# The first 40 microseconds of a two-layer graph kernel: ScalarE normalizes twelve tiles, one token load moves up, and five of GpSimd's loads wait

## The chip, the cores and the metric

The kernel runs on one core of one Trainium2 chip. The core has a matrix engine (TensorE, PE in the profile), a vector engine (VectorE, DVE), a scalar engine (ScalarE, ACT), GpSimd (POOL), a queue engine that only issues transfers here (SyncE, SP), and 16 DMA engines that all transfers share. The metric is the device time of one execution in microseconds (us), lower is better.

## The reference

Two layers are applied to 3327 nodes with 256 features. Each layer has a graph part and a mixture of experts. Only the first graph part matters here:

```python
x = x + relu(adj @ (layernorm(x) @ W) + b)          # layer 0, graph part
x = x + moe0(layernorm(x))                          # top 2 of 8 experts, hidden 1024, relu
x = x + gnn1(layernorm(x), adj)                     # tanh-filtered adjacency, two projections
x = x + moe1(layernorm(x))                          # top 2 of 8 experts, hidden 256, gelu

def layernorm(x, eps=1e-5):
    return (x - mean(x)) / sqrt(var(x) + eps)       # over the 256 features of a node
```

All of it is in float32. `adj` is 3327 x 3327, 44 MB, and is the largest input.

## The kernel before

The nodes are padded to 3328, which is 26 tiles of 128. `x` holds all tiles in SBUF, and `s` holds their normalized copy. The transposed adjacency is read in 13 panels of 256 columns, each in two chunks of 13 tiles (1664 KB); six ring buffers take the chunks. Layer 0 multiplies in the order (adj @ normalized x) @ W. For a panel, TensorE accumulates over the 26 tiles two matmuls per tile (`add`, L381 to L389, one for each half of the features), ScalarE copies the two sums out (L410), TensorE multiplies by W (L396, in `finish`), and VectorE adds the bias `gnn_b_sb` and the residual (`add_relu`, L329 and L330). Then `after0` normalizes the panel's two tiles and routes them to experts, using `gate` (L447).

The first two panels are computed side by side, so that the start has two panels' work for every tile of tokens that arrives: L424 to L426 run over the first 13 tiles and, for each, over both panels. The profile counts two records for each float32 matmul, so a tile with both panels has eight.

**The start.** SP issues the loads in the order of the code: L147 to L153 load the tokens in five groups (tiles 0 and 1, 2 and 3, 4 to 7, 8 to 12, 13 to 25), and behind each of the first four groups the slices of the first chunk of panels 0 and 1 for the same tiles. Next come the second chunks of both panels (L344), W (L417), the gate weights, which are written to DRAM turned (L143), and the chunks of panel 2. Meanwhile 54 small bf16 matmuls run on TensorE (L160).

**Normalizing.** L1111 to L1113 go through six groups of tiles, (0, 2), (2, 2), (4, 4), (8, 4), (12, 6) and (18, 8), each given as first tile and number of tiles. For a group, `statistics` (L267) takes mean and variance of each tile (L275, L276) and then 1/sqrt by a guess and three Newton steps on very short operands (L278 to L287); `layernorm` (L290) then writes each tile of `s` with one VectorE instruction (L297). A group's tiles are ready only after the statistics of all its tiles. The tile framework's scheduler orders the instructions of an engine by priority; `behind` (L231) and `tc.issue_after` set that priority only, they add no wait on the chip. Each engine then works in the order it was given, and each instruction waits by semaphores for its inputs.

**ScalarE at the start.** Apart from the copies it only counts the positive entries of the adjacency: `count` (L1121) runs eight sign instructions per chunk (L1126, 128x416), the first of which waits for the whole first chunk of panel 0.

**GpSimd at the start.** It makes constants and issues six loads: the bias on all partitions (`gnn_b_sb`, 128 KB, L245, called at L253), `f0_bg_sb` (4 KB, L254), and for layer 1 `g1_wg_sb` (256 KB, L1116), `f1_r_sb` (8 KB), `f1_b1_sb` (8 KB) and `g1_bp_sb` (1 KB). Then follow the zeros that `fill` (L1085) needs, and the load of `gate`, 1 MB, each partition getting a copy (L258), which waits until the turned weights are in DRAM. The profile shortens some of the names (`g_wg_sb`, `f_bg_sb`).

Of the kernel before, what the change touches and what calls it, by code (L numbers as in the profile page):

```python
# [10 lines left out]
F32 = mybir.dt.float32  # L11
BF16 = mybir.dt.bfloat16
I32 = mybir.dt.int32
AF = mybir.ActivationFunctionType
ALU = mybir.AluOpType
# [7 lines left out]
P = 128  # L23
NT = 26
NP = NT * P
D = 256
DC = D // P
E = 8
# [4 lines left out]
CJ = NT // NCHUNK  # L33
# [58 lines left out]
def gnn_moe_two_layers(  # L92
# [24 lines left out]
    nc = tc.nc  # L117

    const = ctx.enter_context(tc.tile_pool(name="const", bufs=1))
    state = ctx.enter_context(tc.tile_pool(name="state", bufs=1))  # L120
    work = ctx.enter_context(tc.tile_pool(name="work", bufs=3))
# [5 lines left out]
    x = state.tile([P, NT, D], F32, name="x")  # L127
    s = state.tile([P, NT, D], F32, name="s")
# [5 lines left out]
    def piece(pan, k):  # L134
        return ring[(pan * NCHUNK + k) % RING].rearrange("p (c w) -> p c w", w=PW)
# [4 lines left out]
    def turn_gate(w):  # L140
        g = dram.tile([E, D], F32, name=f"gate{len(gates)}")
        with nc.allow_non_contiguous_dma("a few thousand elements"):
            d = nc.sync.dma_start(out=g.rearrange("e d -> d e"), in_=w)  # L143
        gates.append(g)
        return d

    for t, n in [(0, 2), (2, 2), (4, 4), (8, CJ - 8), (CJ, NT - CJ)]:  # L147
        nc.sync.dma_start(out=x[:, t : t + n, :], in_=x_in[:, t : t + n, :])
        if t < CJ:
            for pan in range(2):  # L150
                nc.sync.dma_start(
                    out=piece(pan, 0)[:, t : t + n, :], in_=adjT[pan, 0, :, t : t + n, :]
                )  # L153

    ones_sq = const.tile([P, P], BF16, name="ones_sq")
    nc.gpsimd.memset(ones_sq, 1.0)
# [2 lines left out]
    for _ in range(WARM):  # L159
# [9 lines left out]
        out=before,  # L169
        in_=before,  # L170
# [56 lines left out]
    def follow(later, earlier):  # L227
        for o in earlier:
            tc.add_manual_dep(later.ins, o.ins.name, after, reason="same rows of DRAM")

    def behind(instructions):  # L231

        if instructions and any(i is instructions[-1].ins for i in nc.cur_bb.bb.instructions):
            return tc.issue_after(instructions[-1].ins)
        return nullcontext()

    def by_feature(name, w, t=None):
        if t is None:
            t = const.tile([P, DC, w.shape[1]], F32, name=name)
        nc.gpsimd.dma_start(out=t, in_=w.rearrange("(c p) n -> p c n", p=P))  # L240
        return t

    def on_all_partitions(name, b):
        t = const.tile([P, b.shape[1]], F32, name=name)
        nc.gpsimd.dma_start(out=t, in_=b.partition_broadcast(P))  # L245
        return t

    def plain(name, a):
        t = const.tile(list(a.shape), F32, name=name)
        nc.gpsimd.dma_start(out=t, in_=a)  # L250
        return t

    gnn_b_sb = on_all_partitions("gnn_b_sb", g0_b[0:1, :])  # L253
    f0_bg_sb = on_all_partitions("f0_bg_sb", f0_bg[0:1, :])  # L254
    gate = state.tile([P, E, D], F32, name="gate")

# [8 lines left out]
    last_normalized = []  # L265

    def statistics(t0, n, kept=None):  # L267


        mv, guess = kept or (  # L270
            work.tile([P, n, 2], F32, name="ln_mv"), work.tile([P, n], I32, name="ln_guess")
        )
        for g in range(n):
            st = work.tile([P, 6], F32, name="ln_st")
            nc.vector.bn_stats(out=st, in_=x[:, t0 + g, :])  # L275
            nc.vector.bn_aggr(out=mv[:, g, :], in_=st)  # L276
        ve = work.tile([P, n], F32, name="ln_ve")
        nc.vector.tensor_scalar(ve, mv[:, :, 1], EPS, None, ALU.add)  # L278
        nw = work.tile([P, n], F32, name="ln_nw")
        half = nw.bitcast(I32)  # L280
        nc.vector.tensor_scalar(half, ve.bitcast(I32), 1, None, ALU.logical_shift_right)
        nc.vector.tensor_scalar(guess, half, -1.0, float(0x5F3759DF), ALU.mult, ALU.add)
        rs = guess.bitcast(F32)
        for _ in range(3):
            nc.vector.scalar_tensor_tensor(nw, rs, -0.5, rs, ALU.mult, ALU.mult)
            nc.vector.tensor_tensor(nw, nw, ve, ALU.mult)
            nc.vector.scalar_tensor_tensor(rs, nw, 1.5, rs, ALU.add, ALU.mult)  # L287
        return mv, rs

    def layernorm(t0, n, stats=None, at=0, xn=None):  # L290


        mv, rs = stats or statistics(t0, n)
        if xn is None:
            xn = work.tile([P, n, K, RW], F32, name="xn")
        for g in range(n):
            last_normalized[:] = [nc.vector.tensor_scalar(  # L297
                xn[:, g, 0, 0:D], x[:, t0 + g, :], mv[:, at + g, 0:1], rs[:, at + g : at + g + 1],
                ALU.subtract, ALU.mult,
            )]  # L300
        return xn
# [24 lines left out]
    def add_relu(x_tile, ps, b_sb):  # L326

        t = work.tile([P, D], F32, name="gnn_t", bufs=2)
        nc.vector.tensor_tensor(t, ps, b_sb, ALU.add)  # L329
        nc.vector.scalar_tensor_tensor(x_tile, t, 0.0, x_tile, ALU.max, ALU.add)  # L330
# [8 lines left out]
    def load_panel(pan, prepare, earlier=(), begun=0):  # L339

        for k in range(begun, NCHUNK):
            a = piece(pan, k)
            with behind(earlier):
                d = nc.sync.dma_start(out=a, in_=adjT[pan, k])  # L344
            last_piece[:] = [d]
            prepare(pan, k, a)
# [24 lines left out]
    def aggregate_first(b_sb, w, w_sb, begin, count, after):  # L371

        sums, waiting, copied = {}, [], []

        def start(pan):
            sums[pan] = [psy.tile([P, PW], F32, name="ps_g", tag="py") for _ in range(DC)]

        def add(pan, j):  # L381
            for c in range(DC):
                nc.tensor.matmul(  # L383
                    sums[pan][c],
                    lhsT=s[:, j, ts(c, P)],
                    rhs=piece(pan, j // CJ)[:, j % CJ, :],
                    start=(j == 0),
                    stop=(j == NT - 1),
                )  # L389

        def finish():
            pan, g = waiting.pop()
            for it in range(PW // P):
                ps = psh.tile([P, D], F32, name="ps_o", tag="ph")
                for c in range(DC):
                    nc.tensor.matmul(  # L396
                        ps, lhsT=g[:, c, ts(it, P)], rhs=w_sb[:, c, :], start=(c == 0),
                        stop=(c == DC - 1),
                    )
                add_relu(x[:, pan * (PW // P) + it, :], ps, b_sb)  # L400
            after(pan)

        def rest(pan, first):
            for j in range(first, NT):
                add(pan, j)
                if waiting and j == first + BEHIND:
                    finish()
            g = work.tile([P, DC, PW], F32, name="xnT", bufs=2)
            for c in range(DC):
                copied.append(nc.scalar.copy(g[:, c, :], sums[pan][c]))  # L410
            waiting.append((pan, g))

        loaded = RING // NCHUNK
        for pan in range(loaded):
            load_panel(pan, lambda pan, k, a: None, begun=1 if pan < 2 else 0)
            if pan == 1:
                nc.sync.dma_start(out=w_sb, in_=w.rearrange("(c p) n -> p c n", p=P))  # L417
                with tc.issue_after(last_piece[0].ins):
                    turn_gate(f0_wgT)
        with tc.issue_after(last_piece[0].ins):  # L420
            turn_gate(f1_rT)
        for pan in range(2):
            start(pan)
        for j in range(CJ):  # L424
            for pan in range(2):
                add(pan, j)  # L426
        for pan in range(NPAN):
            if pan > 1:
                start(pan)
            if loaded < min(pan + RING // NCHUNK, NPAN):  # L430
                load_panel(loaded, lambda pan, k, a: None)
                loaded += 1
            begin(pan)
            count(pan, copied)
            rest(pan, CJ if pan < 2 else 0)
        return finish
# [648 lines left out]
    def fill(*lists):  # L1085


        with tc.issue_after(last_piece[0].ins):
# [13 lines left out]
            for xlist in lists:  # L1102
                for e in range(E):
                    first = xlist[e * NP : e * NP + SB, :].rearrange("(g p) d -> p g d", p=P)
                    nc.sync.dma_start(out=first[:, :, 0:ID], in_=zeros)
                    with nc.allow_non_contiguous_dma("two elements of a partition"):
                        nc.sync.dma_start(
                            out=first[:, :, ID : ID + 1], in_=rows_f[:, e, :].unsqueeze(2)
                        )

    for t0, n0 in [(0, 2), (2, 2), (4, 4), (8, 4), (12, 6), (18, 8)]:  # L1111
        with behind(last_normalized if t0 < 12 else ()):
            layernorm(t0, n0, xn=s[:, t0 : t0 + n0, :].unsqueeze(2))  # L1113

    with tc.issue_after(last_normalized[0].ins):
        g1_wg_sb = by_feature("g1_wg_sb", g1_wg)  # L1116
        f1_r_sb = by_feature("f1_r_sb", f1_rT)
        f1_b1_sb = plain("f1_b1_sb", f1_b1)
        g1_bp_sb = plain("g1_bp_sb", g1_bp)

    def count(pan, copied):  # L1121
        for k in range(NCHUNK):
# [463 lines left out]
```

## Time and profile before

| | us |
|---|---|
| runs shown, median of 4 | 1233.91 (1232.66 to 1238.42) |
| the profiled execution's own time | 1236.28 |
| its span | 1234.6 |
| TensorE busy in the span | 1196.3 (97%) |
| VectorE, ScalarE, GpSimd busy | 708.4, 511.6, 271.1 |
| first float32 matmul | 7.69 |
| tile 12's first matmul | 33.05 |
| W multiplied into panel 0 (first L396) | 51.28 |

Times inside the profile count from the start of the span. A line of the view in order of time gives start, length, engine, source line, operation, the tiles written and read, how often, and in brackets how long the engine had been idle and what it waited for. A line of the view by stretches gives the length, then for PE, PEld (weight loads), DVE, ACT and POOL the busy time and the number of instructions, then the granted TensorE clock (1.00 is full), the share of time in which the 16 DMA engines were busy (which can read a little over 1), and GB/s.

### The profile page before, as it was taken

Reading aid. Unit: us, or ns where it says so; the run is one execution under the profiler, and the core shown is the slowest. Engines: PE = TensorE matmul, PEld = TensorE weight load, DVE = VectorE, ACT = ScalarE, POOL = GpSimd, SP = SyncE. Lnnn points to the kernel's source line nnn. Section 1 sums busy time; section 2 is a strip of 40 time slices with the busy share of each in tenths; the row PEclk is TensorE's granted clock in tenths of the full one; section 3 lists DMA queues with packets and bytes.
Section 4 is the critical chain, followed back from the end, with each engine's and each line's share of the span. In section 5 each row is a group of like instructions: output and inputs, shape, how many; then the busy total and the mean of one; then the engine's idle time right before and its main releaser. Section 6 shows DMA issues by size and latency. Waiting matters only on the chain. (4 is left out here: it accounts for less than half of the span.)

```text
span 1234.6 us, 18156 instructions
## 1 busy us (share of the span) xinstructions
PE 1196.3 (97%) x5819; PEld 1035.4 (84%) x5819; DVE 708.4 (57%) x2841; ACT 511.6 (41%) x950; POOL 271.1 (22%) x341
## 2 busy tenths in 40 slices
PE   8999999999999999999999999999999999989973
PEld 7888888888888888888888888888888888868863
DVE  7577756766682111211111358389999998785454
ACT  2655456446322222223232325994554551033321
POOL 3004112211231111110111110013233232255531
PEclk9999999999999999999999999999999999989986
DMA  9799744443357556657575746234554451568686
GB/s 341 178 310 276 212 163 152 162 165 124 111 191 237 184 189 199 232 177 259 179 248 189 277 168 265 101 138 174 184 178 163 172 199 50 157 191 247 206 267 214
DMA packets 123178, 241.60 MB, mean 196 GB/s; under 512 B 24480, under 2 KB 93120, under 8 KB 116160
## 3 DMA queue, kind: packets, MB, share of 16 engines
q1 hardware_dynamic: 108656, 205.59, 51.2%
q0 software_dynamic: 11136, 31.60, 7.0%
q10 hardware_dynamic: 3280, 3.15, 0.7%
q8 instruction: 48, 0.79, 0.3%
q14 instruction: 58, 0.48, 0.1%
HBM read 203.98 MB, written 36.33 MB: 195 GB/s over the span
## 5 line engine op out<-in xcount | busy, mean ns | idle before, releaser
L383 PE MATMUL ps_g<-ring,s 128*128 128x256 f32 x1352 | 297.0, 381 | 4.3 <-DVE s L297 4.3
L360 PE MATMUL ps_g<-s,ring 128*128 128x256 f32 x1352 | 294.2, 380 | 0.0
L383 PEld LDWEIGHTS ps_g<-ring,s 128*128 128x128 f32 x1352 | 257.0, 191 | 40.1 <-DVE s L297 5.3
L360 PEld LDWEIGHTS ps_g<-s,ring 128*128 128x128 f32 x1352 | 256.0, 190 | 34.4
L941 PE MATMUL ps_h<-xT,ring 128*128 128x256 f32 (+1 forms) x1176 | 252.8, 368 | 4.3 <-ACT xT L932 4.0
L941 PEld LDWEIGHTS ps_h<-xT,ring 128*128 128x128 f32 x1176 | 207.3, 192 | 41.9 <-ACT xT L932 4.4
L948 ACT ACTIVATE wide<-ps_h,ring 128x256 f32<-128x256 f32 (+1 forms) x240 | 110.1, 459 | 285.3 <-PE ps_h L941 265.4
L447 DVE SCALAR_TENSOR_TENSOR rt_product<-xn,gate 128x256 f32<-128x256 f32 x400 | 198.6, 496 | 12.2
L980 PE MATMUL ps_y<-ring,wide 128*128 128x256 f32 x896 | 200.3, 379 | 0.0
L551 POOL DMA_INDIRECT xlist<-xn,rt_idx x104 | 105.1, 1011 | 390.8 <-DVE ln_ve L278 154.0
L980 PEld LDWEIGHTS ps_y<-ring,wide 128*128 128x128 f32 x896 | 167.1, 190 | 21.0
L1126 ACT ACTIVATE sign<-ring,below 128x416 bf16<-128x416 f32 x208 | 133.5, 642 | 9.7 <-DMA ring<-in_adjT 3.5
L551 POOL DMA_INDIRECT ys<-narrow,index x56 | 54.8, 978 | 326.8 <-DVE narrow L988 234.7
L1275 ACT ACTIVATE ring<-ring 128x3328 f32<-128x3328 f32 x22 | 65.4, 2979 | 87.7 <-DVE ring L1274 50.6
L932 DVE COPY xT<-ptb 128x512 f32<-128x512 f32 (+1 forms) x29 | 18.9, 651 | 142.1 <-PE ptb L929 142.1
L987 DVE TENSOR_TENSOR narrow<-ps_y,ring 128x256 f32<-128x256 f32 x56 | 23.8, 424 | 131.7 <-PE ps_y L980 130.3
L512 ACT ACTIVATE rt_d<-rt_d 128x2 f32<-128x2 f32 x26 | 5.3, 203 | 164.2 <-DVE rt_d L511 164.1
L551 POOL DMA_INDIRECT ys<-wide,index x58 | 58.5, 1008 | 67.1 <-DVE wide L988 36.0
L1276 ACT ACTIVATE ring<-ring 128x3328 f32<-128x3328 f32 x22 | 65.4, 2979 | 0.6
L329 DVE TENSOR_TENSOR gnn_t<-ps_o,gnn_b_sb 128x256 f32<-128x256 f32 x26 | 11.0, 424 | 82.4 <-PE ps_o L396 82.4
L980 PE MATMUL ps_y<-s,narrow 128*128 128x256 f32 (+1 forms) x200 | 50.3, 392 | 2.8 <-issue 2.7
L275 DVE BATCH_NORM_STATS2 ln_st<-x 128x6 f32<-128x256 f32 x104 | 42.1, 414 | 6.1 <-DMA x<-in_x 5.5
(213 smaller groups left out, 1039.3 us busy)
## 6 DMA issues: line engine op xcount, KB each, us to landing
ring<-in_adjT SPq DMA_DIRECT2D x50, 1664.0 KB
ring<-in_f_w1T SPq DMA_DIRECT2D x30, 1024.0 KB
ring<-in_f_w2T SPq DMA_DIRECT2D x30, 1024.0 KB
ring<-xlist SPq DMA_DIRECT2D x52, 258.0 KB
ring<-in_f_w SPq DMA_DIRECT2D x36, 256.0 KB
ring<-ys SPq DMA_DIRECT2D x12, 512.0 KB
ring<-in_f_b SPq DMA_DIRECT2D x34, 128.0 KB
xlist<-wide SPq DMA_DIRECT2D x16, 257.0 KB
```

Source lines behind the costliest of these rows:

```text
L275: nc.vector.bn_stats(out=st, in_=x[:, t0 + g, :])
L360: nc.tensor.matmul(ps[it], lhsT=chunks[k][:, c, ts(it, P)], rhs=s[:, j, :], start=(j == 0), stop=(j == NT - 1),)
L383: nc.tensor.matmul(sums[pan][c], lhsT=s[:, j, ts(c, P)], rhs=piece(pan, j // CJ)[:, j % CJ, :], start=(j == 0), stop=(j == NT - 1),)
L447: nc.vector.scalar_tensor_tensor(product, xn[:, g, 0, 0:D], 1.0, gate[:, e, :], ALU.mult, ALU.mult, accum_out=sc[:, g, e : e + 1],)
L551: d = nc.gpsimd.indirect_dma_start(out=a[:, :], out_offset=bass.IndirectOffsetOnAxis(ap=index, axis=0), in_=rows_, in_offset=None,)
L941: nc.tensor.matmul(ps, lhsT=w1[:, c, ts(hc, P)], rhs=xT[:, c, :], start=(c == 0), stop=(c == DC - 1),)
L948: nc.scalar.activation(hT[:, hc, :], ps, func, bias=bb1[:, hc : hc + 1])
L980: last_product[:] = [nc.tensor.matmul(ps, lhsT=hT[:, hc, ts(g, P)], rhs=w2[:, hc, :], start=(hc == 0), stop=(hc == hc_n - 1),)]
L987: nc.vector.tensor_tensor(y[:, g, :], ps, bb2, ALU.add)
L1126: nc.scalar.activation(sign, piece(pan, k)[:, :, ts(i, GROUP)], AF.Sign, bias=below, accum_out=positive[:, pan, i, k : k + 1],)
L1275: nc.scalar.activation(a, a, AF.Square)
L1276: nc.scalar.activation(a, a, AF.Tanh)
```

## The change

There are four edits, all in the first 55 us.

1. SP's order: the tokens of tiles 2 and 3 are issued ahead of panel 1's first slice instead of behind it. Everything else keeps its place.
2. TensorE's order: over the first 13 tiles, panel 0 takes two tiles, then panel 1 takes the same two.
3. For tiles 0 to 11, VectorE computes only the statistics and, once per group, a shift of -mean/std; ScalarE writes the tiles of `s` as scale times x plus shift. Tiles 12 to 25 stay on VectorE. The first ScalarE instruction brings the load of its function table with it, which now waits for the first tokens instead of the adjacency. In ScalarE's order three sign instructions stand between tiles 4 to 7 and tiles 8 to 11, the other five of that chunk behind them.
4. GpSimd's loads: `gnn_b_sb`, `g1_wg_sb`, `f1_r_sb`, `f1_b1_sb` and `g1_bp_sb` get a true dependence on the last normalization instruction of the start (that of tile 25). On GpSimd's queue they now stand behind the `gate` load, in this order, and ahead of the copies for the first token lists. `f0_bg_sb` stays where it was; the zeros of `fill` come earlier.

```diff
-    for t, n in [(0, 2), (2, 2), (4, 4), (8, CJ - 8), (CJ, NT - CJ)]:
+    def load_tokens(t, n):
         nc.sync.dma_start(out=x[:, t : t + n, :], in_=x_in[:, t : t + n, :])
-        if t < CJ:
-            for pan in range(2):
-                nc.sync.dma_start(
-                    out=piece(pan, 0)[:, t : t + n, :], in_=adjT[pan, 0, :, t : t + n, :]
-                )
+    def load_slice(pan, t, n):
+        nc.sync.dma_start(out=piece(pan, 0)[:, t : t + n, :], in_=adjT[pan, 0, :, t : t + n, :])
+
+    first_groups = [(0, 2), (2, 2), (4, 4), (8, CJ - 8), (CJ, NT - CJ)]
+    load_tokens(*first_groups[0])
+    for group, following in zip(first_groups, first_groups[1:]):
+        load_slice(0, *group)
+        if group[0] == 0:
+            load_tokens(*following)
+        load_slice(1, *group)
+        if group[0] > 0:
+            load_tokens(*following)
...
-    gnn_b_sb = on_all_partitions("gnn_b_sb", g0_b[0:1, :])
+    gnn_b_sb = const.tile([P, D], F32, name="gnn_b_sb")
     f0_bg_sb = on_all_partitions("f0_bg_sb", f0_bg[0:1, :])
...
-        for j in range(CJ):
+        for j in range(0, CJ, 2):
             for pan in range(2):
-                add(pan, j)
+                for i in range(j, min(j + 2, CJ)):
+                    add(pan, i)
...
     for t0, n0 in [(0, 2), (2, 2), (4, 4), (8, 4), (12, 6), (18, 8)]:
-        with behind(last_normalized if t0 < 12 else ()):
+        if t0 >= 12:
             layernorm(t0, n0, xn=s[:, t0 : t0 + n0, :].unsqueeze(2))
-    with tc.issue_after(last_normalized[0].ins):
-        g1_wg_sb = by_feature("g1_wg_sb", g1_wg)
-        f1_r_sb = by_feature("f1_r_sb", f1_rT)
-        f1_b1_sb = plain("f1_b1_sb", f1_b1)
-        g1_bp_sb = plain("g1_bp_sb", g1_bp)
+            continue
+        with behind(last_shift):
+            mv, rs = statistics(t0, n0)
+            shift = work.tile([P, n0], F32, name="ln_shift")
+            last_shift[:] = [nc.vector.scalar_tensor_tensor(
+                shift, mv[:, :, 0], -1.0, rs, ALU.mult, ALU.mult
+            )]
+        for g in range(n0):
+            nc.scalar.activation(
+                s[:, t0 + g, :], x[:, t0 + g, :], AF.Identity, bias=shift[:, g : g + 1],
+                scale=rs[:, g : g + 1],
+            )
+    for t, w in [
+        (gnn_b_sb, g0_b[0:1, :].partition_broadcast(P)),
+        (g1_wg_sb, g1_wg.rearrange("(c p) n -> p c n", p=P)),
+        (f1_r_sb, f1_rT.rearrange("(c p) n -> p c n", p=P)),
+        (f1_b1_sb, f1_b1),
+        (g1_bp_sb, g1_bp),
+    ]:
+        follow(nc.gpsimd.dma_start(out=t, in_=w), last_normalized)
```

More of the change, by code (lines that the diff above doesn't have):

```diff
@@ L1109, in fill @@
                         )
+    last_shift = []
     for t0, n0 in [(0, 2), (2, 2), (4, 4), (8, 4), (12, 6), (18, 8)]:
-        with behind(last_normalized if t0 < 12 else ()):
+        if t0 >= 12:
             layernorm(t0, n0, xn=s[:, t0 : t0 + n0, :].unsqueeze(2))
-    with tc.issue_after(last_normalized[0].ins):
-        g1_wg_sb = by_feature("g1_wg_sb", g1_wg)
-        f1_r_sb = by_feature("f1_r_sb", f1_rT)
-        f1_b1_sb = plain("f1_b1_sb", f1_b1)
-        g1_bp_sb = plain("g1_bp_sb", g1_bp)
+            continue
[10 more added lines that the diff above has]
+            )
+    g1_wg_sb = const.tile([P, DC, D], F32, name="g1_wg_sb")
+    f1_r_sb = const.tile([P, DC, E], F32, name="f1_r_sb")
+    f1_b1_sb = const.tile(list(f1_b1.shape), F32, name="f1_b1_sb")
+    g1_bp_sb = const.tile(list(g1_bp.shape), F32, name="g1_bp_sb")
+    for t, w in [
[6 more added lines that the diff above has]
+        follow(nc.gpsimd.dma_start(out=t, in_=w), last_normalized)
     def count(pan, copied):
```

## The prediction

> **What bounds the kernel now.** Read first the busy shares on the page, then who waits for whom, then the first 100 us in order of time, since every edit lies in the first 55 us.
>
> ```profile
> PE 1196.3 (97%) x5819; PEld 1035.4 (84%) x5819; DVE 708.4 (57%) x2841; ACT 511.6 (41%) x950; POOL 271.1 (22%) x341
> ...
> PE ps_g L383 <- DVE s L297: 4.3, 3, 2.1
> ...
> POOL gate L258 <- DMA gate<-in_f_wgT: 30.1, 1, 30.1
> ```
>
> TensorE is the bound. The edits can reach only its start and the three waits for a normalized tile, 4.3 us together. TensorE in order of time (start, length, what, and in brackets the idle time before):
>
> ```profile
> 1.07 4.71 PE L160 MATMUL ps_warm<-ones_sq 128*128 128x128 bf16 x54 [1.07 <-POOL ones_sq L156]
> 7.69 3.72 PE L383 MATMUL ps_g<-ring,s 128*128 128x256 f32 x16 [1.90 <-DVE s L297]
> 13.54 19.22 PE L383 MATMUL ps_g<-ring,s 128*128 128x256 f32 x80 [2.14 <-DVE s L297]
> 33.05 18.40 PE L383 MATMUL ps_g<-ring,s 128*128 128x256 f32 x84 [0.28 <-DVE s L297]
> ```
>
> 16 records are tiles 0 and 1 for both panels, 80 are tiles 2 to 11, and at 33.05 TensorE gets tile 12. After that it has no idle time until far behind panel 0's finish, so **whatever tile 12 gains, the kernel gains**. VectorE says what tile 12 waits for:
>
> ```profile
> 9.70 0.75 DVE L275 BATCH_NORM_STATS2 ln_st<-x 128x6 f32<-128x256 f32 x2 [1.74 <-DMA x<-in_x]
> ...
> 13.08 0.74 DVE L297 TENSOR_SCALAR s<-x,ln_mv,ln_guess 128x256 f32<-128x256 f32 x2
> ...
> 26.31 0.76 DVE L275 BATCH_NORM_STATS2 ln_st<-x 128x6 f32<-128x256 f32 x2 [1.31 <-DMA x<-in_x]
> ...
> 32.58 0.73 DVE L297 TENSOR_SCALAR s<-x,ln_mv,ln_guess 128x256 f32<-128x256 f32 x2
> ```
>
> The last tokens (tiles 13 to 25) land at 26.31; tile 12, one of their group of six, is ready 6.74 us later. VectorE was idle before them, so the transfer decides, not VectorE. TensorE in 13.54 to 32.76 had time to lose: ten tiles at 8 records of 0.217 us (104 take 22.61) are 17.4 us, and they took 19.2, because the clock was halved for a stretch. The stretches around it (length, busy time and count per engine, clock, DMA share, GB/s):
>
> ```profile
> 5.00:6.50 1.50, 0.79 (x15) 0.61 (x11) 1.26 (x8) 0.00 (x0) 1.50 (x7) 1.00 0.43 109
> 6.50:9.50 3.00, 1.81 (x8) 1.63 (x9) 1.31 (x6) 0.00 (x0) 2.98 (x11) 1.00 1.00 254
> 9.50:14.00 4.50, 2.36 (x11) 1.76 (x10) 3.85 (x19) 0.00 (x0) 0.92 (x5) 1.00 1.01 359
> 19.00:26.00 7.00, 7.00 (x34) 6.17 (x33) 5.59 (x27) 6.31 (x15) 0.00 (x0) 1.00 1.03 430
> ```
>
> The transfers ran slowest just when GpSimd's six loads (issued 2.22 to 8.54, 405 KB) were under way.
>
> **The change, part by part.**
>
> *GpSimd's loads.* Five of six leave the start; f0_bg stays. At 389 GB/s (reached in 3.0 to 3.5) the 9 us from 5 to 14 would carry 3500 KB; the three rows carry 164 + 762 + 1616 = 2540. The missing 960 KB are 2.5 us, and the 400 KB that GpSimd itself moved another 1.0. If all that goes, the last tokens land 3.5 us earlier; if only the bytes count, 1.0; if other things slow that stretch, 0. f0_bg still goes through the same queue with its small rows, so I leave 1.1 us of the slow stretch in place: **2.4 us earlier, 23.9**.
>
> The Trainium skill (DMA: Bandwidth & Descriptors, "Issuing engines are not separate DMA queues") says that transfers of all engines share the same 16 DMA engines and interleave. By it alone the gain is the loads' bytes, 1.0 us; the 109 GB/s row with a DMA share of 0.43 says they also cost time in which nothing moved.
>
> Where they go: GpSimd's queue then holds the gate load (it waits until 40.62), gnn_b, the two weights and two biases, then the copies for the token lists. The dependence on the last normalization (36.53 + 2.67 = 39.2 now) is over by then. The five issues are 0.55 to 0.80 us, 3.4 in all; the next of GpSimd's work was at 58.17, so they cost nothing there. g1_wg, f1_r, f1_b1 and g1_bp are for layer 1. gnn_b was used at 52.34, now behind the 1 MB gate load: see the second rival. The fill's zeros move ahead on GpSimd; its stores start at 54.33: nothing.
>
> *Second pair's tokens first.* SP issues them one place earlier; every other transfer keeps its place. They wait for x0 and one 256 KB slice instead of two: at 313 GB/s 0.8 us earlier, and without gnn_b still more. They need only land before VectorE is free at 7.4 to hide; I take that. The second panel's slice becomes fourth; what was fourth landed at 9.70. The new pair order asks for it four matmuls of 0.435 into the work, at 9.8: hidden.
>
> *ScalarE normalizes.* VectorE loses twelve L297 (0.37 of spacing each, 4.4 us) and gets four ln_shift of about 0.17, spacing 0.20. One ScalarE pass with both operands per partition is not in the trace: from below 0.37 (the copy L410, 128x256), from above 0.64 (sign, 128x416); I take 0.55. Its table load (1.28) moves ahead of the first shift: tokens at 3.7, done by 5.0. Group by group, on VectorE's own chains:
> - tiles 0, 1: shift at 7.22 instead of L297; ScalarE 7.45 to 8.0; **TensorE starts at 8.05, 0.36 later** (0.2 to 0.5). Tiles 0, 1 end at 11.5.
> - tiles 2, 3: statistics from 7.42, chain 13.08 - 9.70 = 3.38, shift, ScalarE: 11.6. TensorE's 2.14 wait becomes about 0.1.
> - tiles 4 to 7: from 11.0; chain 17.90 - 13.73 = 4.17; ready 15.95, TensorE free at 15.1: wait 0.85. Up to 2 if these tokens land late.
> - tiles 8 to 11: from 15.4, chain 4.4, ready about 20.6. ScalarE has put three sign passes (2.3) ahead, which wait for the first panel's slice, 19.48 at the latest: ready 22.4 even so. TensorE comes at 22.9: hidden. The other signs end before 30.36, when the next slice came.
> - TensorE is through tile 11 at 22.9 + 6.9 = 29.8, at full clock.
> - tile 12: 23.9 + 6.74 = **30.65** instead of 33.05.
>
> So the wait for tile 12 grows from 0.28 to 0.85, and the gain is 33.05 - 30.65 = **2.4 us**. Its ends: 0 if the last tokens land no earlier, and 33.05 - 29.8 = 3.25 if they land so early that TensorE's own chain decides. The halved clock is part of neither sum: without it, TensorE would have waited for tile 12 all the same.
>
> **Sum.** The profiled execution took 1236.28 (span 1234.6 and 1.7 around it): 1236.3 - 2.4 = 1233.9. It stands 2.4 above the median of the runs shown, 1233.91, so on the median **1231.5**.
>
> **Rivals.**
> - *The clock plays along.* Each time, 3.41 us with TensorE busy 1.43 us or less were followed by 3.41 at half clock (1.27 at 11.18, then 0.51); with 1.52 it stayed full:
>
> ```profile
> 4.35:7.77 3.42, 1.52 (x26) 1.00 0.78 196
> ...
> 11.18:14.59 3.41, 1.27 (x7) 0.99 1.03 374
> 14.59:18.01 3.42, 3.42 (x10) 0.51 1.03 417
> ...
> 1093.21:1096.62 3.41, 1.43 (x8) 0.99 0.56 193
> 1096.62:1100.03 3.41, 2.94 (x9) 0.51 0.79 229
> ```
>
>  A half-clock stretch costs 1.7 us, and at the end of the kernel several waits of this size come against these stretches 2.4 us earlier. One fewer: 1229.8; two: 1228.1. One more: 1233.2. The page can't say which.
> - *gnn_b comes too late (slower).* Panel 0's add (L329) would be at 49.9, the load behind 1 MB of gate. Gate was used at 58.02 without a wait, so it lands somewhere between 41.2 and 58. VectorE idles 5 us at 84.4 to 89.5, and TensorE takes the second pair's choice at 90.13, ready at 82.8: 7.3 us are free. It decides if gnn_b lands after 57; at 63.5 it eats the gain and 4 us more, 1238.
> - *Only bytes count:* tokens at 25.3, tile 12 at 32.05, 1232.9. *Nothing lands earlier:* 1233.9; against it the 109 GB/s row.
> - *The change doesn't do it:* ScalarE's queue could hold a normalization behind a sign; but its order has only tiles 8 to 11 behind signs, with 0.5 us to spare at worst.
>
> **How the numbers follow.** 0.3%, 3.7 us, is about what a measurement of this kernel can tell from no change. The forecast (1230.6 to 1232.3) 0.43; fewer half-clock stretches or a still earlier start 0.27, nearly all below 1230.2; only bytes, or nothing earlier 0.19; gnn_b or another new wait 0.11. Faster 0.27, same 0.63, slower 0.10. The range 1227.8 to 1235.2 leaves the two-stretch end and most of the slow case out.
>
> **What would show it.** The first f32 matmul near 8.05; the waits for tiles 2 and 4 under 1 us; no half clock before 35; the last tokens near 24; tile 12 near 30.7; an L329 wait at panel 0 named for a DMA. Tile 12 at 33, or panel 2's first matmul (65.96 now) not 2 to 3 us earlier, would make this wrong.

## The result, and the profile after

The changed kernel takes 1232.65 us (median of 44 runs, 1229.95 to 1235.63) against 1234.17 for the kernel before on the same chip (70 runs, 1229.51 to 1240.27). The ratio over all runs is 0.9984 (that of the two medians alone is 0.9988), with a 95% interval of 0.9976 to 0.9992: a gain of 1.0 to 3.0 us, clear of zero, but about half of the 0.3% that the prediction counts as no change. The profiled execution took 1233.13, its span 1231.4 (before: 1236.28 and 1234.6).

TensorE in order of time, kernel after (start, length, engine, line, operation, count, and in brackets the idle time before it and what ended that):

```profile
8.09 7.32 PE L391 MATMUL ps_g<-ring,s 128*128 128x256 f32 x32 [1.48 <-ACT s L1133]
17.00 32.21 PE L391 MATMUL ps_g<-ring,s 128*128 128x256 f32 x148 [1.59 <-ACT s L1133]
49.05 1.89 PE L404 MATMUL ps_o<-proj_sb,xnT 128*128 128x256 f32 x8
...
63.73 22.61 PE L391 MATMUL ps_g<-ring,s 128*128 128x256 f32 x104
88.72 1.99 PE L404 MATMUL ps_o<-proj_sb,xnT 128*128 128x256 f32 x8 [2.38 <-ACT xnT L418]
```

The first line is tiles 0 to 3 without a listed wait, the second everything from tile 4 to past panel 0's end: there is no wait for tile 12 any more. W is multiplied into panel 0 at 49.05 instead of 51.28, **2.23 us earlier**, and the stretch with most of panel 2 starts 2.23 earlier too (63.73 against 65.96; the first six tiles of panel 2 lie ahead of it, so 65.96 is not its first matmul, as the prediction calls it). But W is multiplied into panel 2 at 88.72, where it was 88.40: a wait of 2.38 for ScalarE's copy, which the kernel before doesn't have, **takes the whole gain back**. VectorE in order of time says where that comes from:

```profile
11.98 0.75 DVE L283 BATCH_NORM_STATS2 ln_st<-x 128x6 f32<-128x256 f32 x2 [0.98 <-DMA x<-in_x]
...
23.27 0.75 DVE L283 BATCH_NORM_STATS2 ln_st<-x 128x6 f32<-128x256 f32 x2 [2.37 <-DMA x<-in_x]
...
56.96 0.42 DVE L337 TENSOR_TENSOR gnn_t<-ps_o,gnn_b_sb 128x256 f32<-128x256 f32 x1 [20.80 <-DMA gnn_b_sb<-in_g_b]
...
88.01 0.16 DVE L520 TENSOR_TENSOR rt_d<-rt_v 128x2 f32<-128x2 f32 x1
```

The last tokens land at 23.27 (26.31 before). The tokens of tiles 4 to 7 come 0.98 after VectorE is free for them, at 11.98. And panel 0's add waits for the bias until 56.96; before, it ran at 52.34. From there VectorE works without a pause worth naming to the routing difference of panel 1's two tiles at 88.01. ScalarE takes that difference through an exponential. ScalarE in order of time, kernel after:

```profile
88.20 0.20 ACT L521 ACTIVATE rt_d<-rt_d 128x2 f32<-128x2 f32 x1 [10.92 <-DVE rt_d L520]
88.31 0.63 ACT L418 COPY xnT<-ps_g 128x256 f32<-128x256 f32 x2
```

and the same two instructions in the kernel before:

```profile
83.59 0.20 ACT L512 ACTIVATE rt_d<-rt_d 128x2 f32<-128x2 f32 x1 [10.93 <-DVE rt_d L511]
83.70 0.63 ACT L410 COPY xnT<-ps_g 128x256 f32<-128x256 f32 x2
```

ScalarE works its instructions in order, and the exponential stands ahead of the copies of panel 2's sums. VectorE is 4.62 us late at the add (56.96 - 52.34), the exponential 4.61 us late, and the copies follow at once in both kernels. Before, they were done at 84.33, four microseconds ahead of TensorE; now TensorE waits for them.

The transfers, by stretches, kernel after (length; busy time and count of PE, PEld, DVE, ACT, POOL; clock; DMA share; GB/s):

```profile
5.00:6.50 1.50, 1.50 (x19) 1.44 (x17) 1.26 (x8) 0.08 (x1) 1.50 (x8) 1.00 0.56 142
6.50:9.50 3.00, 1.52 (x10) 1.26 (x8) 2.59 (x15) 1.09 (x2) 0.82 (x6) 1.00 0.95 320
9.50:14.00 4.50, 4.50 (x22) 3.75 (x21) 3.21 (x18) 1.09 (x2) 0.00 (x0) 1.00 1.03 422
```

Before they read 109, 254 and 359 GB/s. From 6.5 on the transfers are faster, as forecast; the stretch from 5.0 to 6.5 is still slow, although only the 4 KB of `f0_bg_sb` are left there of GpSimd's loads.

### The profile page after: what moved, and what is told of

Same layout as the page of the kernel before. It is cut to its first block, busy times and chain, and to the rows that moved or that the text cites. A ratio compares the mean times of both kernels' runs of the same rounds, so it can differ in the third digit from the quotient of the medians.

```text
span 1231.4 us, 18169 instructions
## 1 busy us (share of the span) xinstructions
PE 1192.9 (97%) x5819; PEld 1031.5 (84%) x5819; DVE 703.5 (57%) x2833; ACT 517.3 (42%) x962; POOL 269.8 (22%) x341
```

## The experiments

Three questions: what in the four edits makes the start faster, whether the late bias is what takes the gain back, and whether the small load left in the start costs what the five others did. The runs came from three chips. On the first the kernel before takes 1224.59, on the others 1235.18 and 1235.35, so ratios are each against the same chip.

### The bias ahead of the gate, or all of GpSimd's loads at their old place

`gnn_first` lets the bias wait only for the normalization of tiles 12 to 17 and issues it ahead of the 1 MB gate load:

```diff
             layernorm(t0, n0, xn=s[:, t0 : t0 + n0, :].unsqueeze(2))
+            if t0 == 12:
+                with tc.issue_after(last_normalized[0].ins):
+                    follow(
+                        nc.gpsimd.dma_start(out=gnn_b_sb, in_=g0_b[0:1, :].partition_broadcast(P)),
+                        last_normalized,
+                    )
...
-        (gnn_b_sb, g0_b[0:1, :].partition_broadcast(P)),
```

> The changed kernel, but gnn_b's load waits only for the normalization of tile 17 and so stands ahead of the gate load on GpSimd. Theory Q (the 2.2 us won at the start are lost at panel 2, because gnn_b lands late behind gate, VectorE starts panel 0 at 56.96, and ScalarE's Exp for the second pair stands ahead of the copy of panel 2's sums): no wait for gnn_b, the copy of panel 2's sums waits for nothing late, panel 0's W product near 49.1 and panel 2's at 86.2 (88.72 in the changed kernel), and about 2.4 us less than the changed kernel in all, near 1230.2. Rival S (ScalarE's and the transfers' moved work delay the copy anyhow): panel 2's W product stays between 88 and 89, time as the changed kernel, 1232.6.

`loads_early` keeps the first three edits and undoes the fourth:

```diff
-    gnn_b_sb = const.tile([P, D], F32, name="gnn_b_sb")
+    gnn_b_sb = on_all_partitions("gnn_b_sb", g0_b[0:1, :])
...
-    for t, w in [
...
-    ]:
-        follow(nc.gpsimd.dma_start(out=t, in_=w), last_normalized)
+    with tc.issue_after(last_normalized[0].ins):
+        g1_wg_sb = by_feature("g1_wg_sb", g1_wg)
+        f1_r_sb = by_feature("f1_r_sb", f1_rT)
+        f1_b1_sb = plain("f1_b1_sb", f1_b1)
+        g1_bp_sb = plain("g1_bp_sb", g1_bp)
```

> The changed kernel with all of GpSimd's loads at their old place: token order, pair order and ScalarE's normalization remain. Theory L: the last tokens land at 25.5 or later, tile 12 is ready after 32, panel 0's W product at 50.5 to 51.3; no wait at panel 2, its W product at 87.6 to 88.4; time as before to 0.8 us less. Rival V: panel 0's W product at 49 to 49.7, panel 2's at 86.2 to 86.8, 2 us less than before.

`loads_only` is the kernel before with the fourth edit alone (the diff above, the other way round).

> The kernel before with the wait of GpSimd's five loads as the only edit. Theory L (these loads slowed the start, and their delay brings the gain): the last tokens land near 23.3 as in the changed kernel, panel 0's W product comes at 49 to 50 (51.28 before, 49.05 changed); the wait at panel 2 is there as well, its W product at 88.5 to 89. Rival V (ScalarE's taking over the normalization brings it): panel 0's W product at 50.7 or later.

`vector_norm` is the kernel after with VectorE normalizing all tiles, as before:

```diff
-        if t0 >= 12:
+        with behind(last_normalized if t0 < 12 else ()):
             layernorm(t0, n0, xn=s[:, t0 : t0 + n0, :].unsqueeze(2))
-            continue
...
-        for g in range(n0):
-            nc.scalar.activation(
...
```

> The changed kernel with VectorE normalizing the first twelve tiles as before. Theory L: TensorE starts at 7.7, the last tokens land near 23.3, and panel 0's W product is within 1 us of the changed kernel's 49.05; the wait at panel 2 stays (W product 88.5 to 89). Rival V: the waits for tiles 2 and 4 grow by the 0.74 and 1.38 us of VectorE's normalizing passes and panel 0's W product comes at 50.2 or later.

Measured, on one chip:

| | time | ratio (95%) | first f32 matmul | tile 2 / 4 / 12 waits | last tokens | W into panel 0 | into panel 2 | bias used |
|---|---|---|---|---|---|---|---|---|
| `gnn_first` | 1222.38 | 0.9978 (0.9968 to 0.9989) | 7.89 | 0.20 / 1.44 / 0.46 | 24.77 | 49.74 | 86.86 | 50.81 |
| `vector_norm` | 1223.15 | 0.9988 (0.9977 to 0.9999) | 7.52 | 0.30 / 1.22 / 0.85 | 24.67 | 49.64 | 86.76 | 52.28, late |
| `loads_early` | 1224.06 | 0.9992 (0.9981 to 1.0002) | 8.07 | 1.29 / 0.89 / 0.80 | 25.84 | 50.81 | 87.94 | 51.88 |
| `loads_only` | 1224.36 | 0.9993 (0.9983 to 1.0003) | 7.71 | 1.92 / - / - | no wait | 50.53 | 87.66 | 52.28, late |

Three things follow. **The rule for tile 12 holds.** TensorE and VectorE of `gnn_first`, in order of time:

```profile
31.51 18.40 PE L391 MATMUL ps_g<-ring,s 128*128 128x256 f32 x84 [0.46 <-DVE s L305]
49.74 1.89 PE L404 MATMUL ps_o<-proj_sb,xnT 128*128 128x256 f32 x8
```

```profile
24.77 0.75 DVE L283 BATCH_NORM_STATS2 ln_st<-x 128x6 f32<-128x256 f32 x2 [3.92 <-DMA x<-in_x]
```

24.77 + 6.74 = 31.51; the other two with a wait for tile 12 give 24.67 + 6.74 = 31.41 (31.40 seen) and 25.84 + 6.74 = 32.58 (32.58 seen). **ScalarE's normalization brings nothing here.** `vector_norm` and `gnn_first` differ by 0.10 us at panel 0, and their times can't be told apart; TensorE starts 0.37 later with ScalarE (the prediction said 0.36). The two also differ in when the bias is issued (38.76 and 33.38), but that comes behind tile 12. **In two kernels the bias was late on this chip too, at 52.28, but cost nothing**: panel 2's product followed panel 0's by 37.12 or 37.13 us in all four kernels. For `vector_norm` and `loads_only` a wait at panel 2 had been expected, and it didn't come. `gnn_first`, with the order of the kernel after and the bias in time, has none either, which speaks against rival S. The kernel after itself was not run on this chip, so the 2.4 us in all that were expected of `gnn_first` can't be read off.

`loads_early` came out as its theory L had it. Beside it, on the same chip, moving the five loads brings the last tokens 1.07 to 1.17 us earlier (24.77 and 24.67 against 25.84) and panel 0 by as much. That is hardly more than the 1.0 us that the prediction gave for the loads' bytes alone.

`loads_only` moved nothing at panel 0 (50.53, where 49 to 50 was expected; the kernel before has 50.39 and 50.21 on the other chips), though its transfers ran at 313 GB/s from 6.5 to 9.5. Its tokens for tiles 2 and 3 still landed at 9.50, TensorE waited 1.92 for them, and a stretch of half clock from 14.2 to 17.6 took the place of the wait for tile 4. So moving five loads away isn't enough as long as the second pair's tokens come late. With the first two edits as well (`vector_norm`), panel 0 ends 0.89 earlier.

### How late may the bias be?

`gnn_later` chains three loads on GpSimd, gate, then `g1_wg_sb` when the gate has landed, then the bias when that has landed:

```diff
+            if pan == 0:
+                last = load_gate(gates[0])
+                for t, src in [
+                    (g1_wg_sb, g1_wg.rearrange("(c p) n -> p c n", p=P)),
+                    (gnn_b_sb, g0_b[0:1, :].partition_broadcast(P)),
+                ]:
+                    d = nc.gpsimd.dma_start(out=t, in_=src)
+                    follow(d, [last])
+                    last = d
```

> The changed kernel with gnn_b made later on purpose: it is issued only when g1_wg has landed, and that only when gate has landed. Theory Q: gnn_b is used at 58 to 62, and the copy of panel 2's sums and with it the W product of panel 2 are late one for one: 88.7 plus the lateness beyond 56.96, so 90 to 94, and the whole kernel 3 to 6 us slower than with gnn_b in time. Rival S: panel 2's W product stays where the changed kernel has it, since VectorE's slack takes the delay.

The kernel after was run again beside it:

> The changed kernel once more, beside the ones below. Theory Q (how late gnn_b lands decides whether panel 2 waits): if it is used at about 52.3, as it was with the loads alone and with VectorE's normalization, panel 2's W product follows panel 0's by 37.1 as in the kernel before and nothing is lost; if near 57, by 39.5 with a 2.4 us wait for the copy. Rival S (the wait belongs to this kernel's own order): the wait at panel 2 is there in either case.

and so was the kernel before:

> The kernel before once more, for its profile on the same chip: panel 0's W product at 51.3 and panel 2's at 88.4 if the start does not differ between chips; up to 1 us otherwise.

`gnn_later` took 1256.18, a ratio of 1.0165 (1.0133 to 1.0198), `after_again` 1234.01, 0.9984 (0.9967 to 1.0001), both against 1235.18. TensorE of `after_again`:

```profile
49.06 1.89 PE L404 MATMUL ps_o<-proj_sb,xnT 128*128 128x256 f32 x8
...
86.96 1.99 PE L404 MATMUL ps_o<-proj_sb,xnT 128*128 128x256 f32 x8 [0.61 <-ACT xnT L418]
```

and its VectorE:

```profile
55.22 0.42 DVE L337 TENSOR_TENSOR gnn_t<-ps_o,gnn_b_sb 128x256 f32<-128x256 f32 x1 [18.70 <-DMA gnn_b_sb<-in_g_b]
```

The bias came 1.74 us earlier than in the first profile of the same kernel, and the wait at panel 2 is 1.77 us shorter. TensorE of `gnn_later`:

```profile
48.76 1.89 PE L404 MATMUL ps_o<-proj_sb,xnT 128*128 128x256 f32 x8
...
74.62 3.75 PE L404 MATMUL ps_o<-proj_sb,xnT 128*128 128x256 f32 x8 [12.75 <-DVE gnn_t L337]
...
105.79 3.78 PE L404 MATMUL ps_o<-proj_sb,xnT 128*128 128x256 f32 x8 [3.88 <-ACT xnT L418]
```

Its bias was used at 74.05, where 58 to 62 was expected. The loss is larger than expected also because a second wait comes in: panel 1's product waits 12.75 for a buffer that panel 0's add has not emptied, and the long idle time is followed by half clock (13.65 us from 66.9, 6.83 from 104.4). All profiles give one rule. Panel 2's product can't start before the add plus 88.72 - 56.96 = 31.76, nor before panel 0's product plus 88.40 - 51.28 = 37.12 (as long as panel 1's doesn't wait):

| | bias used | + 31.76 | panel 0's product | + 37.12 | panel 2's product, seen |
|---|---|---|---|---|---|
| after | 56.96 | 88.72 | 49.05 | 86.17 | 88.72 |
| `after_again` | 55.22 | 86.98 | 49.06 | 86.18 | 86.96 |
| `gnn_later` | 74.05 | 105.81 | 48.76 | - | 105.79 |
| `vector_norm` | 52.28 | 84.04 | 49.64 | 86.76 | 86.76 |
| `loads_only` | 52.28 | 84.04 | 50.53 | 87.65 | 87.66 |
| before | 52.34 | 84.10 | 51.28 | 88.40 | 88.40 |

The later of the two is what is seen, within 0.02 (the two numbers were taken from the first and the last row). The eight profiles that the table leaves out fit too, within 0.01. The bias becomes dear once it is used later than 5.36 us after panel 0's product, in the kernel after at 54.41. Issued behind the gate, it was used at 56.96 and 55.22 in the kernel after and at 52.28 in both kernels on the 1224 us chip. Those two leave the normalization to VectorE, so whether the chip or the kernel makes this difference wasn't separated.

The second profile of the kernel before corrects the starting point. Its TensorE:

```profile
13.53 3.72 PE L383 MATMUL ps_g<-ring,s 128*128 128x256 f32 x16 [1.75 <-DVE s L297]
18.34 32.21 PE L383 MATMUL ps_g<-ring,s 128*128 128x256 f32 x148 [1.09 <-DVE s L297]
50.39 1.89 PE L396 MATMUL ps_o<-proj_sb,xnT 128*128 128x256 f32 x8
```

This execution had no half clock in the start and no wait for tile 12: VectorE took up its last tokens at 24.89 without waiting for them, and TensorE's own chain set panel 0's end, at 50.39. A third one (`before_third`, below) has the last tokens at 25.24 and 50.21. So 0.9 to 1.1 us of the 2.23 gained between the first two profiles belong to that one execution of the kernel before, whose last tokens landed only at 26.31, and the gain at panel 0 against the other two is **1.2 to 1.3 us**.

### The 4 KB load that was left in the start

`both_biases_late` is `gnn_first` with `f0_bg_sb` treated in the same way, so that no load of GpSimd is left in the first 30 us:

```diff
-    f0_bg_sb = on_all_partitions("f0_bg_sb", f0_bg[0:1, :])
+    f0_bg_sb = const.tile([P, E], F32, name="f0_bg_sb")
...
+                    follow(
+                        nc.gpsimd.dma_start(out=f0_bg_sb, in_=f0_bg[0:1, :].partition_broadcast(P)),
+                        last_normalized,
+                    )
```

> As with gnn_b ahead of gate, and f0_bg taken out of the start too, so that GpSimd issues no load in the first 30 us. Theory G (GpSimd's loads in the start are what slows the transfers from 5 to 9.5 us, even f0_bg's few bytes): those 4.5 us carry over 300 GB/s, the last tokens land near 22.5 and TensorE's own chain decides: panel 0's W product at 48.3 to 48.8. Rival B (the stretch is slow by itself; only bytes count): the last tokens stay near 24.7, panel 0's W product near 49.7.

It ran a second time on another chip:

> The kernel with both biases late (no GpSimd load in the first 30 us) once more, beside the next two. Panel 0's W product near 47.6 and panel 2's 37.1 later, 0.3 to 0.4% less than before.

`vector_biases_late` is the same with VectorE normalizing all tiles:

> The same with VectorE normalizing the first twelve tiles. Theory P (with the transfers out of the way, TensorE waits for the chains of VectorE, and the 0.74 and 1.38 us of passes taken off it count): panel 0's W product 0.5 to 1.5 us later than the run beside it, 48.1 to 49.1. Rival N (the passes taken off VectorE come back as the second hop and the longer ScalarE pass): within 0.3 us of it.

`loads_in_time` is the kernel before with all six loads moved in this way and none of the other three edits:

> The kernel before, its only edit that no load of GpSimd starts in the first 30 us, with both biases ahead of gate; token order, pair order and VectorE's normalization as before. Theory G (GpSimd's loads are the main thing): panel 0's W product at 48.5 to 49.5, no wait at panel 2, 2 us or more below before. Rival O (the second pair's tokens being behind the second panel's slice costs as much): 50 or later.

and the kernel before ran beside them a third time:

> The kernel before, for its profile beside these: panel 0's W product at 50.4 if no half clock falls into the first 35 us, near 51.3 if one does.

| | time | ratio (95%) | 5.0 to 6.5, GB/s | 6.5 to 9.5, GB/s | W into panel 0 | into panel 2 |
|---|---|---|---|---|---|---|
| `both_biases_late` | 1230.96 | 0.9970 (0.9953 to 0.9987) | 296 | 368 | 47.63 | 84.76 |
| `both_biases_again` | 1232.79 | 0.9978 (0.9963 to 0.9994) | 326 | 390 | 48.60 | 85.73 |
| `vector_biases_late` | 1232.88 | 0.9981 (0.9968 to 0.9995) | 348 | 382 | 48.41 | 85.54 |
| `loads_in_time` | 1233.58 | 0.9977 (0.9963 to 0.9990) | 279 | 391 | 48.62 | 85.75 |
| `after_again` | 1234.01 | 0.9984 (0.9967 to 1.0001) | 96 | 329 | 49.06 | 86.96 |
| `before_again`, `before_third` | 1234.21, 1236.59 (one run each) | | 115, 132 | 251, 269 | 50.39, 50.21 | 87.51, 87.34 |

The stretches of `both_biases_late`:

```profile
5.00:6.50 1.50, 1.50 (x19) 1.42 (x17) 1.25 (x8) 0.00 (x0) 1.37 (x10) 1.00 0.94 296
6.50:9.50 3.00, 1.69 (x9) 1.44 (x8) 2.64 (x15) 1.09 (x2) 0.18 (x1) 1.00 0.97 368
```

and its TensorE in order of time:

```profile
7.90 7.17 PE L391 MATMUL ps_g<-ring,s 128*128 128x256 f32 x32 [1.31 <-ACT s L1143]
15.59 32.21 PE L391 MATMUL ps_g<-ring,s 128*128 128x256 f32 x148 [0.51 <-ACT s L1143]
47.63 1.89 PE L404 MATMUL ps_o<-proj_sb,xnT 128*128 128x256 f32 x8
...
84.76 1.89 PE L404 MATMUL ps_o<-proj_sb,xnT 128*128 128x256 f32 x8
```

All ten profiles with `f0_bg_sb` in the start show 96 to 143 GB/s from 5.0 to 6.5, whether the five other loads were there or not; the four without it 279 to 348. GpSimd is busy with small instructions in either case (1.50 us of these 1.50 with it, 1.37 to 1.39 without), so that isn't what differs. **It isn't the loads' bytes that slow this stretch; even the smallest of them, alone, does it.** Without it the last tokens land at 22.30 and 21.90, the wait for tile 4 falls to 0.51 or to nothing, panel 0's product comes 2.76 us ahead of `before_again`, and the 2.75 are kept at panel 2, where nothing waits.

SP's issues in order of time show one step more. First the kernel after, then `both_biases_late`; in each the second line is the issue of the last tokens:

```profile
4.11 2.88 SPq L151 DMA_DIRECT2D ring<-in_adjT  x2
...
10.05 0.33 SPq L148 DMA_DIRECT2D x<-in_x  x1
```

```profile
4.10 1.09 SPq L151 DMA_DIRECT2D ring<-in_adjT  x2
...
7.97 0.33 SPq L148 DMA_DIRECT2D x<-in_x  x1
```

The two issues from 4.1 took 2.24 to 3.19 us in the ten profiles with `f0_bg_sb` in the start and 1.09 to 1.18 in the four without, and everything that SP issues behind them comes later. Whether the load holds up SP's issues, or these wait for transfers that it slows, isn't shown.

`loads_in_time` shows how much of the gain is the loads alone. Its TensorE:

```profile
11.76 3.72 PE L383 MATMUL ps_g<-ring,s 128*128 128x256 f32 x16 [0.30 <-DVE s L297]
16.58 32.21 PE L383 MATMUL ps_g<-ring,s 128*128 128x256 f32 x148 [1.10 <-DVE s L297]
48.62 1.89 PE L396 MATMUL ps_o<-proj_sb,xnT 128*128 128x256 f32 x8
```

The wait for tile 2 is down to 0.30 with the old token order as well, and panel 0's product is 1.59 us ahead of `before_third`, as theory G had it. The two reorderings add nothing that can be seen: `vector_biases_late` is 0.21 ahead at panel 0 (48.41 against 48.62), but by the same 0.21 already at the first matmul (7.53 against 7.74). ScalarE's normalization adds 0.78 at most (48.41 to 47.63 on another chip, a wait of 0.51 instead of 1.10 for tile 4). In `both_biases_again`, the run beside `vector_biases_late`, it is -0.19: 48.60, where 47.6 was expected, with a half-clock stretch at 7.9. By the times, these four can't be told apart. TensorE of `both_biases_again` shows the one chain from start to past panel 0's end:

```profile
8.14 40.63 PE L391 MATMUL ps_g<-ring,s 128*128 128x256 f32 x180 [2.31 <-ACT s L1143]
```

`before_third` had a half-clock stretch from 8.0, and its panel 0 still comes at 50.21, where 51.3 had been expected with one. `loads_only` had one from 14.2, close to where the first profile of the kernel before has it (14.6), and 50.53. So it was the late tokens of that first profile that put its panel 0 at 51.28, and not the clock.

`both_biases_late` has the lowest ratio of all, and it is faster than both kernels' medians on its chip (1230.96 against 1235.18 and 1234.01). Its interval overlaps that of the kernel after, so against that one the step is likely, not shown.

## Why the prediction was right, and where it was not

1231.5 was forecast and 1232.65 measured, in the range and within 0.3% of before, the likeliest class. Step by step:

- **The last tokens 2.4 us earlier: 3.04 between the two profiles (26.31 to 23.27).** Right in kind, but the reference was an unlucky one: `before_third` had them at 25.24, which leaves 1.6 to 2.0, and side by side on one chip the five loads made 1.07 to 1.17. So the term was sized too large, and for these five loads the rival "only bytes count" (1.0) is not ruled out by when the tokens land; against it speak only the rates, 320 and 422 GB/s from 6.5 to 14 where they were 254 and 359, with 400 KB less to move. For `f0_bg_sb` it is ruled out: 4 KB less took the stretch from 5.0 to 6.5 from 96 to 296 GB/s on one chip. The Trainium skill (DMA: Bandwidth & Descriptors, "Issuing engines are not separate DMA queues") has the transfers of all engines interleave on the same 16 DMA engines. That alone doesn't give the price of this small load.
- **"I leave 1.1 us of the slow stretch in place", for `f0_bg_sb`:** right that it stays slow; it was nearly all of the stretch that stayed. The part taken out came behind 6.5.
- **Tile 12 decides, at 30.65:** half failed. It decides at 6.74 after the last tokens where it decides (three kernels to 0.01), but in the kernel after it doesn't: the tokens were so early that TensorE's own chain came later, at 17.00 + 64 records of 0.217 = 30.9. The end named for that, 29.8, was missed by the wait for tile 4, forecast at 0.85 "up to 2 if these tokens land late"; it was 1.59, and they did: VectorE began them at 11.98 instead of 11.0.
- **"The halved clock is part of neither sum":** right for the one profile that it was read from, where tile 12 wasn't ready before 33.05 in any case. What failed is that profile as a starting point: its last tokens came at 26.31, in `before_again` by 24.89 and in `before_third` at 25.24. In these two panel 0 ended 0.89 and 1.07 us earlier, and the forecast should have taken a gain of some 1.3 at panel 0.
- **TensorE starts 0.36 later:** 0.40 in the profile (7.69 to 8.09), 0.37 in the pair that in the start differs in this alone. **ScalarE's pass at 0.55:** the first two took 1.09 together. **Tile 2's wait about 0.1:** none listed, and the 32 records took 7.32, 0.15 more than the shortest seen (7.17). **Second pair's tokens in time:** VectorE began them at 7.47 without waiting.
- **"7.3 us are free" for the bias: failed**, and this is the step that changes what happens. The mechanism of that rival was seen, the bias behind 1 MB of gate, but its slack was read off VectorE's idle time and TensorE's need of the choice at 90.13. A third way to TensorE was overlooked: ScalarE's in-order queue has the exponential ahead of the copies that panel 2 needs. The point from which it decides is 54.41, not 57, and at 56.96 it cost 2.55 (88.72 - 86.17), more than the whole gain, and in the second profile 0.8 of 1.3.
- **The sign "2 to 3 us earlier" at 65.96:** 63.73, so 2.23 against that profile, but only 1.34 and 1.16 against the two others of the kernel before (65.07 and 64.89).

So at panel 2 the kernel after stands at 88.72 and 86.96, the kernel before at 88.40, 87.51 and 87.34: one of its two profiles is later than all three of the kernel before, the other 0.4 to 1.4 us earlier. In these profiles the difference in time lies behind the start of layer 1 (its first transposes at 732.71 and 731.11, before at 732.24, 731.56 and 731.36): from there to the end of the span it takes 498.7 and 500.2 us after, 502.4, 500.8 and 503.5 before. In that part half-clock stretches lie between waits, the rival "the clock plays along"; the profiles with the longer rest have more of them (before has them at 1097, 1107, 1206 and two in a row from 1179, after at 1099 and 1204). With two each, `after_again` and `before_again` are only 0.6 us apart there. That the change removes such stretches wasn't shown by any run, and two profiles against three don't settle it. **The size of the forecast came out; that the gain of the start reaches the end didn't**, and that the number was met is by these profiles in part luck.

Also open: by what a load of 4 KB by GpSimd slows all transfers from 5.0 to 6.5; why the bias behind the gate is used at 52.28 in two kernels on one chip and at 55.22 and 56.96 in the kernel after elsewhere; and why the last tokens land at 24.67 and 24.77 on that chip, and at 23.27 to 23.80 elsewhere, with the same five loads moved.

## What to carry to other kernels

When a load is moved behind others, follow its consumer's result through every in-order queue to the next instruction that the bound engine needs: the slack is the shortest of these ways, not the idle time of the first consumer, and the gain ahead of it shortens it by as much. Take two or three profiles of the kernel before, before a wait of a microsecond is booked as a gain: nearly half of this one was in one execution only. And take the smallest load out of a crowded start as well as the large ones, since what it cost here was not in its bytes.

## What the runs showed of the hardware that was not expected

- One 4 KB load issued by GpSimd held the transfers of the whole core at 96 to 143 GB/s from 5.0 to 6.5 us; without it they ran at 279 to 348. With it, two issues by SP took 2.24 to 3.19 us, without it 1.09 to 1.18.
- A 256 KB load that GpSimd issued alone at 53.60 in `gnn_later` took over ten microseconds to land, while SP issued the stores of the zeros for the token lists. GpSimd in order of time:

```profile
53.60 0.72 POOL L426 DMA_DIRECT2D g_wg_sb<-in_g_wg  x1 [12.56 <-DMA gate<-gate]
64.91 0.56 POOL L426 DMA_DIRECT2D gnn_b_sb<-in_g_b  x1 [10.59 <-DMA g_wg_sb<-in_g_wg]
```

- The same kernel had a half-clock stretch of 3.41 us in its start in some executions and not in others: before at 14.6, at 8.0 or nowhere, `both_biases_late` nowhere, its repetition at 7.9. At 8.0 it cost the kernel before nothing, since the wait for tile 2 shrank from 1.75 to 0.19.
- One chip ran the same program 0.9% faster than the two others (1224.59 against 1235.18 and 1235.35).
